# A four-part model on one core: feed-forward norms summed on ACT, a quantiser that takes the maximum twice, a column ahead of the gates, and a new plan

## The chip, the cores and the metric

The kernel runs on one core of a Trainium2 chip. The metric is the time on the device in microseconds (us), median of a few runs. The core's engines work side by side, each through its own list of instructions in order: PE (matrix products; PEld is its loading of weights), DVE (vector), ACT (functions of single elements), POOL (general), and SP, which here only issues the transfers (DMA). PE writes its results to PSUM, a small memory of eight banks of 128x512 floats; all else lives in SBUF. An engine waits for another at semaphores.

## The reference

The input x is 16 sequences of 512 tokens with 128 channels, in float32. Four residual blocks follow each other, each on the layer norm of x (mean and variance over the 128 channels).

```python
x = x + _L0_attn_a_ref(_layernorm(x), ...)   # four layers of RWKV
x = x + _L0_ffn_ref(_layernorm(x), w_gate, w_up, w_down)
x = x + _L0_attn_b_ref(_layernorm(x), w_qkv, w_out, b_out)   # causal attention, one head of 64
x = x + _L0_ffn_ref(_layernorm(x), w_gate, w_up, w_down)
```

An RWKV layer has a time mix and a channel mix. In the time mix k, v and a gate r are products of mixtures of a token and the one before it; per channel a recurrence over the tokens keeps a running weighted mean of v:

```python
qq = jnp.maximum(pp, ww)
e1, e2 = jnp.exp(pp - qq), jnp.exp(ww - qq)
out = (e1 * aa + e2 * vv) / (e1 * bb + e2)
```

The channel mix squares the relu of a 128 to 512 product, goes back to 128, and gates it. The feed-forward block rounds the inputs of every product to a 4-bit grid, in blocks of 16 along the last axis:

```python
scale = jnp.maximum(jnp.max(jnp.abs(xb), axis=-1, keepdims=True) / 6.0, 1e-12)
idx = jnp.searchsorted(_MID, jnp.abs(xb / scale))
q = _GRID[idx] * jnp.sign(xb / scale) * scale       # grid 0, .5, 1, 1.5, 2, 3, 4, 6
h = jax.nn.silu(fp4_linear(x, w_gate)) * fp4_linear(x, w_up)     # 352 wide
return fp4_linear(h, w_down)
```

## The kernel before

All of x stays in SBUF. A sequence is a tile of 128 tokens by 4 blocks of 128 channels. The stages are `in` (load and the two first norms), `x0` to `x3` (the four RWKV layers, two sequences at a time, eight groups), `ffn1`, `att`, `ffn2` (one sequence at a time) and `out`; `w0` to `w3` and `wf` prepare weights. Each stage of each group is a generator that yields operations with their tiles; where an operation can run on several engines it yields alternatives.

The order on every engine is written by a planner in the kernel, at build time. `Issue.merge` keeps up to 8 generators (`ACTIVE`) in play and picks one operation after the other, by a start time that it works out from cost formulas (in `tt`, `ts`, `act` and others), hop times between engines and free buffers, shifted by ranks of the stages (`RANK`), leads of kinds of operations (`LEAD`), ages and a seeded jitter (`SEEDS`). The result is a fixed program order for each engine; at run time only semaphores wait. Tiles come from pools: `slots` (s, 128x513), `wides` (w, 128x1028), `tinys` (t, statistics and scales) and eight PSUM banks (ps).

Three places matter here.

`ln_stats` takes the sums for a layer norm. DVE takes `bn_stats` of each 128x128 block, small operations combine them, POOL raises the variance to the power -0.5 (`power`), and `normalise` applies scale and bias, on POOL or ACT. A second way lies in the function behind `scratch`: ACT sums x and then the squares of x minus its mean through the accumulator of its activations; DVE scales both.

`quant` rounds to the grid: the maximum of each block of 16, its reciprocal, a product on POOL, then rounding by adding and subtracting a large number (`MAGIC`, or a multiple of the value, `ABOVE`): ACT takes the multiple and a Relu of it less `MAGIC`, DVE adds and subtracts in two passes, and POOL multiplies by the scale. `ffn` calls it on 128x512 for x and on 128x704 in two parts of 352 for h.

`time_mix` computes the recurrence as scans on DVE. In the last of them the weights are s = 0.5 - 0.5 tanh(...) of the token before, and it scans over differences of v plus bias from one token to the next. Tile `t2` holds the tanh and later v, `a2` the differences and the result.

Line numbers of the profile that are helpers: L431 `mm`, L434 `tp` (transposes), L366 `act`, L340 `tt`, L344 `stt`, L355 `ts`, L335 `power`, L409 `scan`, L413 `reduce_max`, L419 `bn_stats`, L425 `memset`, L376 `copy`. Since one line serves many steps, groups are told apart by tile names and shapes.

Of the kernel before, what the change touches and what calls it, by code (L numbers as in the profile page):

```python
# [10 lines left out]
F32 = mybir.dt.float32  # L11
# [3 lines left out]
AF = mybir.ActivationFunctionType  # L15
# [8 lines left out]
D = 64  # L24
# [10 lines left out]
N_SLOT = 22  # L35
N_TINY = 12
# [9 lines left out]
AGE = 15.97  # L46
SWITCH = 89.0

FIRST = 45770.0
AGE_FIRST = 19.9  # L50
AGE_LAST = 9.79
LAST = 7
# [4 lines left out]
    882, 832, 99, 213, 457, 65, 500, 631, 716, 630, 411, 526, 117, 14, 667, 453, 213, 800, 28, 513, 118, 323, 14, 553,  # L57
    825, 916, 944, 652, 176, 713, 814, 499, 482,
# [9 lines left out]
WEIGHT = {"V": 2.491, "A": 0.666, "P": 0.962, "T": 1.0, "D": 1.0, "L": 0.1}  # L68
# [9 lines left out]
    "A ps<-ps 251": -70.2, "A ps<-ps 438": 10.4, "A ps<-ps 571": 66.4, "A ps<-ps,x 571": 1.0, "A ps<-s 199": 98.1, "A ps<-s 386": 59.3,  # L78
    "A ps<-s 519": 35.0, "A ps<-w 386": -10.5, "A ps<-w 518": -28.1, "A s,t<-ps,t 344": 44.6, "A s,t<-ps,t 451": 8.1, "A s,t<-ps,t 557": 80.1,
    "A s,t<-ps,t 664": -29.3, "A s<-ps 158": 6.6, "A s<-ps 265": -24.8, "A s<-ps 371": -35.8, "A s<-ps 478": -13.6, "A s<-ps 663": -94.0,  # L80
    "A s<-s 519": -64.5, "A s<-x,t,t 385": -157.7, "A w<-ps 345": 30.5, "A w<-ps 571": 21.8, "A w<-ps,x 571": 19.8, "A w<-s 519": -103.2,
    "A w<-w 1038": -45.5, "A w<-w 944": -102.7, "A w<-w 945": -29.7, "A x<-ps 131": -19.2, "A x<-ps 158": -51.1, "A x<-s 199": -34.4,
    "A x<-s 519": 2.9, "A x<-s,t,t 385": -60.5, "A x<-x 199": -49.8, "A x<-x 519": -15.8, "D <-x 873": 15.5, "D s<- 430": 88.9, "D s<- 600": -20.0,
    "D s<- 873": -0.5, "D x<- 430": 51.2, "D x<- 873": 50.8, "P s<- 205": -44.8, "P s<-s,s 1226": -38.8, "P s<-s,t 1082": 88.5, "P s<-s,t 353": 32.2,
    "P s<-s,t 778": 27.3, "P s<-x,t,t 426": 28.5, "P t<-t 1634": 7.7, "P t<-t 942": -9.6, "P t<-t,t 158": 12.7, "P t<-t,t 167": 22.1,
    "P w<- 42": 38.0, "P w<-s,w 1226": 50.0, "P w<-w,t 1447": 19.3, "P w<-w,w 1223": 135.0, "P w<-w,w 152": -129.2, "P w<-w,w 2342": 43.2,
    "P w<-x 205": 58.4, "P x<-s,t,t 426": 23.4, "P x<-s,x 1226": 77.6, "P x<-s,x 389": -58.1, "P x<-x 1226": 77.2, "P x<-x 426": 11.9,
    "P x<-x 714": 32.8, "P x<-x,s 1226": 2.1, "P x<-x,x 1082": 39.6, "T ps<- 110": 58.7, "T ps<-s 110": -3.8, "T ps<-s 222": 95.6,
    "T ps<-s,s 110": -22.4, "T ps<-s,s 125": 48.3, "T ps<-s,s 179": -47.5, "T ps<-s,s 222": 21.3, "T ps<-s,s 232": 35.4, "T ps<-s,x 222": -107.1,
    "T ps<-s,x 592": 18.2, "T ps<-w 110": -49.3, "T ps<-w,x 222": 6.6, "T ps<-x,s 859": -13.0, "T ps<-x,w 232": -40.0, "V ps<-ps,w 1130": -121.8,  # L90
    "V ps<-w,ps 602": -29.7, "V s<-ps,s 203": 129.0, "V s<-ps,s 436": 116.3, "V s<-ps,s 603": -30.8, "V s<-ps,s 664": -66.8, "V s<-s 197": 41.2,
    "V s<-s,ps 203": 74.3, "V s<-s,ps 436": 35.3, "V s<-s,ps 603": 21.0, "V t<-ps 203": -3.0, "V t<-ps 336": -3.6, "V t<-ps 470": 54.2,
    "V t<-ps 603": 27.2, "V t<-s 202": -45.8, "V t<-s 203": -8.6, "V t<-s 436": 48.3, "V t<-s 603": -12.1, "V t<-t 120": 18.9, "V t<-t 207": 17.1,
    "V t<-t 270": 29.9, "V t<-t 345": -4.3, "V t<-t 70": 49.5, "V t<-t 74": 46.9, "V t<-t 81": 23.7, "V t<-t 86": 54.8, "V t<-t 92": -18.5,
    "V t<-t 95": -69.9, "V t<-t,t 74": 37.1, "V t<-t,t 78": 19.2, "V t<-w 803": -116.6, "V t<-x 202": -43.8, "V w<-ps 1130": -106.2,
    "V w<-ps,w 1130": 44.4, "V w<-ps,w 436": -41.7, "V w<-ps,w 603": -43.4, "V w<-ps,w 664": -21.7, "V w<-s 336": -11.8, "V w<-w 662": -15.3,
    "V w<-w,ps 436": -34.2, "V w<-w,ps 602": -6.0, "V w<-w,w 71": -10.9, "V x<- 70": 23.1, "V x<-ps 71": -21.7, "V x<-ps,t,x 264": -79.9,
    "V x<-s 136": -43.6, "V x<-s 336": -11.0, "V x<-x 136": -11.5, "V x<-x 336": 12.9, "V x<-x 603": 49.6, "V x<-x 71": 1.7, "V x<-x,ps 603": -76.8,
    "V x<-x,x 603": 76.5,
# [5 lines left out]
    "warm": (-2, 0), "in": (-0.806, 0.421), "w0": (-0.644, 0), "w1": (0.622, 0.147), "w2": (1.351, 0.081), "w3": (1.608, 0), "wf": (2.286, 0),  # L105
    "x0": (-0.078, 0), "x1": (1.222, 0), "x2": (2.04, 0), "x3": (3.568, 0), "ffn1": (3.742, 0.485), "att": (5.354, 0.494), "ffn2": (6.262, 0.674),
    "out": (7.177, 0.552),
# [5 lines left out]
LN_ACT = False  # L113
# [89 lines left out]
class View:  # L203


    def __init__(self, buf, steps=()):
        self.buf, self.steps = buf, steps
        a = self._at(buf.tile)
        self.shape = a.shape
        row = a.ap[0][0]  # L210
        self.lo = a.offset % row if row else 0
        self.spread = any(st == 0 and n > 1 for st, n in a.ap[1:])
        self.hi = self.lo + sum(st * (n - 1) for st, n in a.ap[1:])
        if buf.psum:

            self.lo, self.hi = 0, 1 << 20
# [48 lines left out]
def in_psum(v):  # L265
    return isinstance(v, View) and v.buf.psum
# [41 lines left out]
class Issue:  # L308
# [28 lines left out]
    def tt(self, e, out, a, b, op):  # L337
        n = width(out)
        cost = 70 + 1.042 * n if e == "V" else 110 + (1.9 if any(isinstance(v, View) and v.spread for v in (a, b)) else 2.18) * n + 40 * (n < 64)
        return self.op(e, cost, out, (a, b), lambda: self.eng(e).tensor_tensor(real(out), real(a), real(b), op))  # L340
# [5 lines left out]
    def ts(self, e, out, a, s0, s1, op0, op1=None):  # L346
        n = width(out)
        ptr = is_ap(s0) + is_ap(s1)
        if e == "V":
            cost = 70 + (1.042 if in_psum(a) or in_psum(out) else 0.52) * n + 61 * ptr  # L350
        else:
            cost = (330 + 0.75 * n) if op0 == ALU.mult else 200 + 2.7 * n
        args = (op0,) if op1 is None else (op0, op1)
        two = not in_psum(a) and not in_psum(out)
        return self.op(e, cost, out, (a, s0, s1), lambda: self.eng(e).tensor_scalar(real(out), real(a), real(s0), real(s1), *args), two_port=two)  # L355

    def act(self, out, a, func, bias=None, scale=None, accum=None, note=None, after=()):
        n = width(out)
        cost = (52 if in_psum(a) else 93) + 0.833 * n + 93 * (is_ap(bias) + (is_ap(scale) and not callable(scale)) + is_ap(accum))
        kw = {k: v for k, v in (("bias", bias), ("scale", scale), ("accum_out", accum)) if v is not None}  # L360
        outs = [out] + ([accum] if accum is not None else [])

        def call():
            if note:
                note()
            return self.nc.scalar.activation(real(out), real(a), func, **{k: v() if callable(v) else real(v) for k, v in kw.items()})  # L366

        return self.op("A", cost, outs, (a, bias, scale), call, func.name, after=after)
# [329 lines left out]
class Net:  # L698
# [133 lines left out]
    def time_mix(self, l, xs):  # L832
# [53 lines left out]
        yield S.act(t2.v.flat, c.v.flat, AF.Tanh, scale=0.5, bias=mw)  # L886
# [5 lines left out]
        for j, x in enumerate(xs):  # L892
            if DIFF:

                v, vb = self.ps(), t2[:, j, :]
                p = self.ps()
                sv = p[:, 1:T]
                if not S_LATE:
                    yield S.act(sv, t2[:, j, 0 : T - 1], AF.Copy, scale=-0.5, bias=0.5, after=(c.v,))
                yield from self.project(v.v, W["Wv"], hds[j], after=(c.v,))  # L900
                if S_LATE:
                    vb = self.slot()[:, 0:T] if S_LATE == 2 else vb
                    yield S.act(sv, t2[:, j, 0 : T - 1], AF.Copy, scale=-0.5, bias=0.5, after=(v.v,))
                yield S.act(vb, v.v, AF.Identity, bias=W["bias"][:, 0:1])
                yield Free(v)
                yield S.add("dv", a2[:, j, 1:], t2[:, j, 1:], t2[:, j, 0 : T - 1], ALU.subtract)
                yield S.small(a2[:, j, 0:1], t2[:, j, 0:1], t2[:, j, 0:1], ALU.add)
                yield S.scan(sv, sv, a2[:, j, 1:], 0.0, ALU.mult, ALU.add)
                yield S.stt(sv, to[:, j, 1:], -1.0, sv, ALU.add, ALU.mult)
                yield S.stt(a2[:, j, 1:], t2[:, j, 1:], 2.0, sv, ALU.mult, ALU.add)  # L910
# [195 lines left out]
    def quant(self, v, xn, tiny, parts):  # L1106
# [13 lines left out]

        at = 0
        for n in parts:
# [3 lines left out]
            yield S.act(cc, cc, AF.Relu, bias=self.nmagic[0:p])  # L1126
            yield S.stt(xp, cc, MAGIC, xp, ALU.add, ALU.add)
            yield S.stt(xp, xp, -MAGIC, cc, ALU.add, ALU.subtract)
# [196 lines left out]
def block_kernel(ctx, tc, a, out):  # L1325
# [20 lines left out]
    k.nmagic = k.const.tile([128, 1], F32, name="nmagic")  # L1346
    nc.vector.memset(k.nmagic, -MAGIC)
# [99 lines left out]
```

## Time and profile before

| what | value |
|---|---|
| time, median of 3 runs | 1418.98 us (1418.74 to 1421.64) |
| the profiled execution | 1421.8 us, span 1420.0 us |
| mean granted PE clock | 0.986 |
| PE, DVE, ACT, POOL busy | 1336.0, 1329.2, 1270.6, 1138.0 us |
| instructions | 25100 |
| DMA | 18.48 MB, 13 GB/s in the mean |

The page gives busy time and share by engine, then forty slices of the span, the DMA queues, the chain of work that ended last, and the costliest groups of instructions. In a group, the two numbers after the bar are busy us and the mean ns of one instruction; after the next bar stands the engine's idle time before them and who ended it. The mean duration of an instruction and the time until the next one starts differ, since an engine overlaps neighbours. Transfers take 4% of the DMA engines' time and are spread over the first 35 us, the loading of later weights, x again for the residual after `x3`, and the output.

### The profile page before, as it was taken

The page shows a single profiled execution, that of the slowest core. Times are in us where ns is not written, and L with a number is a line of the kernel's source. Part 1 is how long each engine was busy: PE and PEld are TensorE (multiplying, and loading weights), DVE is VectorE, ACT ScalarE, POOL GpSimd, SP SyncE. Part 2 cuts the span into 40 slices and gives each one's busy share as a digit, 9 for nine tenths or more (in the row PEclk, how much of TensorE's full clock was granted, in tenths as well). Part 3 has the DMA queues.
Part 4 walks back from the last instruction along what each step waited for, and adds up shares of the span by engine and source line. Part 5 has one row for each costly group of instructions (what it writes and reads, how often), then busy time and mean ns, then how long its engine had stood idle before and what let it go on. Part 6 is the DMA issues. An engine that isn't in the chain of part 4 may idle for free.

```text
span 1420.0 us, 25100 instructions
## 1 busy us (share of the span) xinstructions
PE 1336.0 (94%) x8219; PEld 1115.9 (79%) x8219; DVE 1329.2 (94%) x3378; ACT 1270.6 (89%) x2350; POOL 1138.0 (80%) x1653
## 2 busy tenths in 40 slices
PE   1589999999999999999999999999999999999988
PEld 1368888888888888888888888888777776777766
DVE  8999999999999999999989999888999999899997
ACT  5889999999999999998999999988888898788885
POOL 7989897887778889787698877988778777677775
PEclk9799999999999999999999999999999999899998
DMA  5000000000000000000000000001000000000001
GB/s 160 1 15 2 0 2 1 1 3 10 14 13 6 3 1 24 1 1 1 1 1 1 16 16 23 24 16 31 1 1 1 1 16 1 15 1 24 8 16 45
DMA packets 31330, 18.48 MB, mean 13 GB/s; under 512 B 1568, under 2 KB 30176, under 8 KB 31200
## 3 DMA queue, kind: packets, MB, share of 16 engines
q1 hardware_dynamic: 31200, 16.89, 4.1%
q8 instruction: 65, 1.06, 0.3%
q14 instruction: 65, 0.53, 0.1%
HBM read 12.69 MB, written 4.19 MB: 12 GB/s over the span
## 4 chain that ended last, share of the span: by engine, by line
PE 57%; DVE 21%; ACT 16%; issue 2%; POOL 2%; SPq 1%; DMA 0%; DVEq 0%; ACTq 0%; POOLq 0%
PE ps L431 51%; ACT s L366 7%; PE ps L434 6%; DVE w L344 4%; ACT ps L366 4%; ACT w L366 3%; DVE w L409 3%; DVE w L340 2%; DVE s L344 2%; DVE t L419 2%; ACT L366 2%; DVE ps L409 1%; DVE t L344 1%; DVE t L413 1%; DVE x L340 1%
## 5 line engine op out<-in xcount | busy, mean ns | idle before, releaser
L366 ACT ACTIVATE s<-ps 128x512 f32<-128x512 f32 (+4 forms) x592 | 330.4, 581 | 46.9 <-PE ps L434 27.5
L431 PE MATMUL ps<-Wcv,s 128*128 128x128 f32 x2048 | 279.7, 275 | 1.2 <-ACT s L366 1.1
L355 POOL TENSOR_SCALAR s<-x,t 128x128 f32<-128x128 f32 x556 | 251.6, 464 | 34.5 <-DVE t L344 15.8
L431 PEld LDWEIGHTS ps<-Wcv,s 128*128 128x128 f32 x2048 | 266.0, 192 | 15.3 <-ACT s L366 2.4
L340 POOL TENSOR_TENSOR w<-w,t 128x704 f32<-128x704 f32 x128 | 176.8, 1388 | 45.2 <-DVE w L344 13.2
L431 PE MATMUL ps<-w,Wck 128*128 128x512 f32 x768 | 207.3, 407 | 4.1 <-DVE w L344 1.5
L335 POOL TENSOR_TENSOR t<-t,nhalf 128x8 f32<-128x8 f32 (+1 forms) x120 | 171.9, 1435 | 41.3 <-DVE t L344 40.0
L434 PE MATMUL ps<-ident,s 128*128 128x128 f32 x873 | 158.9, 280 | 35.3 <-ACT s L366 21.5
L431 PEld LDWEIGHTS ps<-w,Wck 128*128 128x128 f32 x768 | 137.3, 189 | 43.0 <-POOL w L340 5.4
L419 DVE BATCH_NORM_STATS2 t<-x 128x6 f32<-128x128 f32 x704 | 160.4, 277 | 0.4
L366 ACT ACTIVATE s<-s 128x512 f32<-128x512 f32 x248 | 156.3, 637 | 1.5
L434 PEld LDWEIGHTS ps<-ident,s 128*128 128x128 f32 x873 | 107.9, 143 | 58.5 <-ACT s L366 27.5
L366 ACT ACTIVATE ps<-w 128x511 f32<-128x511 f32 (+1 forms) x256 | 134.9, 535 | 7.6 <-POOL w L340 3.3
L431 PE MATMUL ps<-w,Wk 128*128 128x512 f32 x384 | 130.5, 434 | 4.3 <-DVE w L344 4.3
L344 DVE SCALAR_TENSOR_TENSOR w<-ps,w 128x352 f32<-128x352 f32 (+1 forms) x192 | 108.8, 569 | 13.4 <-ACT ps L366 12.0
L431 PE MATMUL ps<-w,Wv 128*128 128x512 f32 x384 | 117.6, 418 | 3.5 <-DVE w L340 3.5
L340 POOL TENSOR_TENSOR x<-x,s 128x512 f32<-128x512 f32 x80 | 103.4, 1295 | 18.0 <-DVE s L344 10.5
L431 PE MATMUL ps<-w,Wr 128*128 128x512 f32 x384 | 114.1, 419 | 1.9 <-DVE w L344 1.8
L344 DVE SCALAR_TENSOR_TENSOR w<-w,ps 128x352 f32<-128x352 f32 (+1 forms) x192 | 107.8, 565 | 1.1
L431 PE MATMUL ps<-wd,s 128*128 128x128 f32 (+1 forms) x768 | 106.6, 278 | 2.4 <-ACT s L366 2.2
L431 PEld LDWEIGHTS ps<-wd,s 128*128 128x128 f32 (+1 forms) x768 | 96.1, 191 | 12.4 <-ACT s L366 5.6
L431 PE MATMUL ps<-wg,s 128*128 128x352 f32 x256 | 100.5, 475 | 3.9 <-ACT s L366 3.7
(143 smaller groups left out, 3439.7 us busy)
## 6 DMA issues: line engine op xcount, KB each, us to landing
s<-in_x SPq DMA_DIRECT2D x32, 256.0 KB, 3.1
out<-x SPq DMA_DIRECT2D x16, 256.0 KB, 2.3
s<-in_Wck SPq DMA_DIRECT2D x4, 256.0 KB, 3.4
Wcv<-in_Wcv SPq DMA_DIRECT2D x4, 256.0 KB, 3.2
s<-in_Wk SPq DMA_DIRECT2D x4, 64.0 KB, 2.2
s<-in_Wv SPq DMA_DIRECT2D x4, 64.0 KB, 2.4
s<-in_Wr SPq DMA_DIRECT2D x4, 64.0 KB, 2.0
Wo<-in_Wo SPq DMA_DIRECT2D x4, 64.0 KB, 3.4
```

The costliest lines, as they stand in the source:

```text
L335: return self.op("P", 250 + 173 * width(out), out, (a,), lambda: self.nc.gpsimd.tensor_tensor(real(out), real(a), half, ALU.pow), brief=True)
L340: return self.op(e, cost, out, (a, b), lambda: self.eng(e).tensor_tensor(real(out), real(a), real(b), op))
L344: return self.op("V", cost, out, (a, s, b), lambda: self.nc.vector.scalar_tensor_tensor(real(out), real(a), real(s), real(b), op0, op1))
L355: return self.op(e, cost, out, (a, s0, s1), lambda: self.eng(e).tensor_scalar(real(out), real(a), real(s0), real(s1), *args), two_port=two)
L366: return self.nc.scalar.activation(real(out), real(a), func, **{k: v() if callable(v) else real(v) for k, v in kw.items()})
L409: return self.op("V", cost, out, (a, b), lambda: self.nc.vector.tensor_tensor_scan(real(out), real(a), real(b), init, op0=op0, op1=op1))
L413: return self.op("V", cost, out, (a,), lambda: self.nc.vector.tensor_reduce(real(out), real(a), AX.X, ALU.max, **kw))
L419: return self.op("V", 202, out, (a,), lambda: self.nc.vector.bn_stats(real(out), real(a)))
L431: return self.op("T", cost, out, (lhsT, rhs), lambda: self.nc.tensor.matmul(real(out), lhsT=real(lhsT), rhs=real(rhs), start=start, stop=s ...
L434: return self.op("T", 110, out, (a,), lambda: self.nc.tensor.transpose(real(out), real(a), ident), after=after)
```

## The change

Four things, in one edit.

1. `LN_ACT` becomes true: the norms of both feed-forward stages take the way behind `scratch`. For a sequence ACT does four Identity passes with an accumulator, DVE scales the sums, ACT does four Square passes with bias and accumulator, DVE scales those, POOL takes the power, DVE multiplies. The four `bn_stats` and the small operations after them go. The normalised tile serves as scratch.
2. In `quant` the Relu on ACT goes (and the constant `nmagic`). Both DVE passes compute max(multiple, `MAGIC`) minus the value.
3. In `time_mix` the tanh is written into `t2` with one column ahead of each sequence, which POOL sets to 1.0. The PSUM tile of s, the differences, the scan and the two products then run over all 512 columns, and the separate addition that made column 0 of the result goes.
4. The pools have one slot and three tinys more, some cost formulas and all parameters of the plan have other values, so the whole program order is another, and so is the choice of engine where there are alternatives.

```diff
-N_SLOT = 22
-N_TINY = 12
+N_SLOT = 23
+N_TINY = 15
...
-AGE = 15.97
-SWITCH = 89.0
+AGE = 17.82
+SWITCH = 108.0
...
-WEIGHT = {"V": 2.491, "A": 0.666, "P": 0.962, "T": 1.0, "D": 1.0, "L": 0.1}
+WEIGHT = {"V": 1.726, "A": 1.05, "P": 0.639, "T": 1.0, "D": 1.0, "L": 0.1}
...
-LN_ACT = False
+LN_ACT = True
...
-        cost = (52 if in_psum(a) else 93) + 0.833 * n + 93 * (is_ap(bias) + (is_ap(scale) and not callable(scale)) + is_ap(accum))
+        base = (43 if in_psum(out) else 68) if in_psum(a) else 76 if in_psum(out) else 106
+        cost = base + 0.833 * n + 93 * (is_ap(bias) + (is_ap(scale) and not callable(scale))) + 18 * is_ap(accum)
...
-        yield S.act(t2.v.flat, c.v.flat, AF.Tanh, scale=0.5, bias=mw)
+        if DIFF:
+
+            ahead = View(t2)[:, 0 : G * (T + 1)].rearrange("p (g t) -> p g t", g=G)
+            yield S.memset("P", ahead[:, :, 0:1], 1.0)
+            yield S.act(ahead[:, :, 1 : T + 1], c.v, AF.Tanh, scale=0.5, bias=mw)
...
-                yield S.act(vb, v.v, AF.Identity, bias=W["bias"][:, 0:1])
-                yield Free(v)
-                yield S.add("dv", a2[:, j, 1:], t2[:, j, 1:], t2[:, j, 0 : T - 1], ALU.subtract)
-                yield S.small(a2[:, j, 0:1], t2[:, j, 0:1], t2[:, j, 0:1], ALU.add)
-                yield S.scan(sv, sv, a2[:, j, 1:], 0.0, ALU.mult, ALU.add)
-                yield S.stt(sv, to[:, j, 1:], -1.0, sv, ALU.add, ALU.mult)
-                yield S.stt(a2[:, j, 1:], t2[:, j, 1:], 2.0, sv, ALU.mult, ALU.add)
+                yield S.act(vb, v.v, AF.Identity, bias=W["bias"][:, 0:1])
+                yield Free(v)
+                yield S.add("dv", a2[:, j, :], vb, ahead[:, j, 0:T], ALU.subtract)
+                yield S.scan(p.v, p.v, a2[:, j, :], 0.0, ALU.mult, ALU.add)
+                yield S.stt(p.v, to[:, j, :], -1.0, p.v, ALU.add, ALU.mult)
+                yield S.stt(a2[:, j, :], vb, 2.0, p.v, ALU.mult, ALU.add)
...
             yield S.act(cc, xp, AF.Abs, scale=ABOVE)
-            yield S.act(cc, cc, AF.Relu, bias=self.nmagic[0:p])
-            yield S.stt(xp, cc, MAGIC, xp, ALU.add, ALU.add)
-            yield S.stt(xp, xp, -MAGIC, cc, ALU.add, ALU.subtract)
+            for _ in range(2):
+                yield S.stt(xp, cc, MAGIC, xp, ALU.max, ALU.subtract)
```

## The prediction

> **What bounds the kernel now.** I read the busy times first, then the chain of work that ended last, then busy time in three stretches, then the groups by shape, and last the order of time on one engine.
>
> ```profile
> PE 1336.0 (94%) x8219; PEld 1115.9 (79%) x8219; DVE 1329.2 (94%) x3378; ACT 1270.6 (89%) x2350; POOL 1138.0 (80%) x1653
> ```
>
> Four engines are between 80% and 94% busy, so no single one explains the time. The chain's shares by engine:
>
> ```profile
> PE 57%; DVE 21%; ACT 16%; issue 2%; POOL 2%; SPq 1%; DMA 0%; DVEq 0%; ACTq 0%; POOLq 0%
> ```
>
> TensorE leads, but DVE and ACT hold over a third. I cut the span at two marks: 306.0 us, where DVE starts the 25th of 64 scans `w<-wdec,ps` (one for each layer and sequence), and 971.5 us, its last `s<-ps,nowr,s` (last channel mix). The columns are length, then PE, PEld, DVE, ACT, POOL busy.
>
> ```profile
> 0.00:306.00 306.00, 251.81 (x1452) 209.73 (x1453) 296.55 (x774) 268.47 (x453) 263.27 (x415) 0.97 0.08 21
> 306.00:971.50 665.50, 655.89 (x4195) 570.96 (x4194) 617.13 (x1359) 630.56 (x1064) 540.65 (x833) 1.00 0.03 10
> 971.50:1420.00 448.50, 428.34 (x2575) 335.19 (x2573) 415.54 (x1248) 371.56 (x835) 334.11 (x407) 0.98 0.04 12
> ```
>
> In A (0 to 306) DVE is busy 97% and PE 82%: DVE sets the pace. In B (to 971.5) PE is busy 98.6%: PE. In C (to the end) PE shows 95.5%, DVE 92.7%; but PE's rows overlap, and priced by step (below) its work in C is only 381 us of 448.5. There DVE's 417 is the largest load, and neither ACT nor POOL is near.
>
> The groups that the change touches (count, then busy us, mean ns):
>
> ```profile
> L419 DVE BATCH_NORM_STATS2 t<-x 128x6 f32<-128x128 f32 x704 | 160.4, 277 | 0.4
> L366 ACT ACTIVATE s<-s 128x512 f32<-128x512 f32 x248 | 156.3, 637 | 1.5
> L366 ACT ACTIVATE ps<-ps,nmagic 128x352 f32<-128x352 f32 x129 | 67.9, 529 | 1.7
> L340 DVE TENSOR_TENSOR w<-w 128x1 f32<-128x1 f32 x48 | 25.1, 523 | 2.8 <-ACT w L366 2.6
> L366 ACT ACTIVATION_READ_ACCUMULATOR s<-ps,t 128x1 f32 x64 | 13.1, 204 | 0.0
> L366 ACT ACTIVATE ps<-ps,nmagic 128x512 f32<-128x512 f32 x32 | 21.4, 668 | 0.3
> L340 POOL TENSOR_TENSOR s<-s 128x512 f32<-128x512 f32 x8 | 8.3, 1042 | 2.4 <-ACT s L366 2.3
> ```
>
> A mean duration overstates what an instruction occupies, since neighbours overlap. So I price by the step from a start to the next start where the engine does not idle:
>
> ```profile
> 1036.77 1.11 DVE L344 SCALAR_TENSOR_TENSOR x<-ps,t,x 128x128 f32<-128x128 f32 x4
> 1037.81 0.27 DVE L344 SCALAR_TENSOR_TENSOR t<-t 128x4 f32<-128x4 f32 x2
> 1038.01 0.86 DVE L419 BATCH_NORM_STATS2 t<-x 128x6 f32<-128x128 f32 x4
> 1038.82 0.95 DVE L340 TENSOR_TENSOR w<-w,ps 128x352 f32<-128x352 f32 x2
> ```
>
> ```profile
> 1046.22 0.54 ACT L366 ACTIVATE ps<-ps,nmagic 128x352 f32<-128x352 f32 x1
> 1046.66 0.51 ACT L366 ACTIVATE s<-x,t 128x128 f32<-128x128 f32 x1
> ...
> 1059.35 0.37 ACT L366 ACTIVATE s<-ps,t 128x128 f32<-128x128 f32 x1
> 1059.61 0.19 ACT L366 ACTIVATION_READ_ACCUMULATOR s<-ps,t 128x1 f32 x1
> 1059.71 0.46 ACT L366 ACTIVATE s<-ps,t 128x256 f32<-128x256 f32 x1
> ```
>
> Four statistics take 0.81 us: 0.20 each. The Relu takes 0.44 (0.45 over all), and reading an accumulator adds 0.10 to its activation, not the 0.204 of its row.
>
> **The change part by part.** Counts are differences of the two programs' instructions by engine; steps are means over the timeline of before.
>
> *Feed-forward norms.* DVE loses 128 statistics: 128 x 0.20 = 25.6 us. Of its `t<-t 128x4` arithmetic it keeps 64 fewer, x 0.12 = 7.5, and gains 16 small adds, 1.9. ACT gains 128 Identity and 128 Square passes over 128x128, each with an accumulator read. No row shows this from SBUF. The nearest: an SBUF copy of 128x128 (`Wr<-s`) steps 0.21, a pointer bias adds 0.09 (`ps<-ps,nmagic` 0.45 against 0.36 for `w<-ps`, both 128x352), the read 0.10. So 0.31 and 0.40, together 91 us. Bounds: reads wholly hidden 65, whole durations instead of steps (0.30 and 0.39, plus 0.204) 141. I take 91, since the timeline shows the 0.10. The upper end would put ACT in C (below) at 408 instead of 367 us, 4 over DVE: +4 us on the time; the lower end changes nothing.
>
> *Quantiser.* ACT loses the Relu: 129 x 0.45 + 32 x 0.57 = 76 us. DVE's two passes stay two, of the same shapes; the second now reads PSUM first, 0.44 against 0.43: nothing. A maximum might price otherwise than an addition; no row shows a difference between ALU operations (`s<-s,ps` with add and multiply and `s<-ps,s` with two additions, both 128x512, both step 0.60), so 0.
>
> *Column ahead.* The 64 column-0 adds go, 48 of them on DVE, where they step 0.485 in the mean: 23.3 us (one lasts 4.32 us, the shortest 0.14). The lower bound is 48 x 0.07 = 3.4, if the wait in them only moves to the next instruction. I take 23, because what follows them, scans and PSUM arithmetic, has no such tail in the trace (`w<-wdec,ps` 1185 to 1219 ns, `w<-ps,w` 665 to 692). They lie in A (17) and B (31), so the lower bound would cost A some 7 us. The 32 new memsets on POOL step 0.08: 2.5. Scans and products grow by one column of 511: nothing.
>
> *New plan.* 46 squares go from ACT (0.52, 24 us) to POOL (1.02, 47 us), and 29 normalisations from ACT (0.39, 11 us) to POOL (0.43, 12 us). POOL's small adds fall by 69 (14 us). SP issues the same 92 rows, but thirteen x loads instead of two now precede layer 1's weights, which are used only when layer 0 has finished for a group; layer 0's work hides it, and without that cover one such load of 2.0 to 3.4 us would be exposed.
>
> Totals: DVE 25.6 + 7.5 - 1.9 + 23.3 = 54 less; ACT 76 + 24 + 11 - 91 = 20 less; POOL some 48 more; PE the same 5,860 program instructions.
>
> POOL's addition is where a rule speaks against the change. DVE's small `t<-t` operations step 0.14 for 128x8 and 0.12 for 128x4 against a shortest 0.08; 565 of them step about 31 us more in all than at their shortest. The Trainium skill (SBUF — State Buffer, Who interferes with whom) says that a DVE instruction with two SBUF inputs contends with a GpSimd instruction that reads SBUF. By it, POOL's 4% more work lengthens those waits by 4%, an estimate of 1.3 us on DVE; by the rows alone nothing is added.
>
> *By stretch.* I weighted the instructions of both programs up to the same marks with these steps (PE: 0.237 for a 128x512 pass, 0.222 for 128x128 in its two rows, 0.593 for 128x352, 0.110 for a transpose).
>
> - A: DVE 292 to 297, because work from behind the mark (three more `w<-ps,w`, two `w<-w,wdec`, two norm products and the like) fills the 8 us of column adds that vanish; PE 226 to 239, so PE arrives 13 us of work further. DVE sets A: 306 + 5 = 311 us. POOL's 8 us more has 43 us of idle time to go into.
> - B: PE 668 to 645, DVE 597 to 552, ACT 588 to 557, POOL 488 to 518. PE sets B: 665.5 x 645/668 = 643 us. DVE's and ACT's relief is worth nothing here.
> - C: DVE 417 to 404 (20 less for statistics, 5 for small arithmetic, some more quantiser work that B had), PE 381 to 391, ACT 358 to 367, POOL 341 to 348. If DVE's losses stay, 448.5 - 13 = 435.5. PE comes close behind, so of its 10 us more between nothing and all come back; I take half: 440 us.
>
> Sum 311 + 643 + 440 = 1394, 26 less than the span of 1420.0. The profiled execution took 1421.8 us, 2.8 over the median of 1418.98; so 1418.98 - 26 gives 1393 us.
>
> **The rivals.**
>
> *Slower: ACT and DVE wait for each other in the new norms.* Each of 32 norms has DVE scale ACT's sums, ACT square with that, DVE scale again: 64 times DVE's queue can stop for ACT, and the quantiser's passes and PSUM products queue behind it; PE waits for those. Rows of such waits (`DVE w L344 <- ACT ps L366: 12.0, 21, 1.7`) give 0.57 us each: 64 x 0.57 = 36 in C, so 1429. It decides from 26/64 = 0.41 us each. Against it: eight threads are interleaved, and DVE now idles 34 of C's 448 us for everything together.
>
> *C does not shorten.* If C's losses come from dependencies of single sequences and not from DVE's load, C stays at 448.5 plus 5: 311 + 643 + 453.5 gives 1408, or 1407 by the median. For it: PE's own idle rows in C name ACT more than DVE.
>
> *The plan's gain in B is not there.* PE's 13 us of lead at 306 is spent again on waits, B stays 665.5: 311 + 665.5 + 440 = 1416.5, within 0.2% at 1415.5 or a little more.
>
> *Better than forecast.* PE's lead shows in A as well (DVE loses its idle 9 us) and C, too, is filled to 97% by DVE's load, 416 us: 302 + 643 + 416 = 1361, 1360 by the median. Against it: PE's 391 us there would also have to run at 94%, where it now has 85%.
>
> **How the numbers follow.** 0.2% (2.8 us) is what a measurement can tell from no change. Forecast 0.50 (1380 to 1404); C not shorter 0.17; better 0.11; B without gain 0.07, of which 0.05 within 0.2%; slower 0.15. Faster: 0.50 + 0.17 + 0.11 + 0.02 = 0.80; same 0.05; slower 0.15. The range takes in the better case down to 1370 and C not shorter, and reaches to 1424 into the slower one; that leaves out 0.12 above and 0.05 below.
>
> **What would show it.** DVE busy near 1275, no `w<-w 128x1` row, 576 statistics `t<-x`; 128 + 128 accumulating activations with a READ_ACCUMULATOR step near 0.10; POOL near 1185; PE's work unchanged; the last `s<-ps,nowr,s` near 954 us. The forecast is wrong if DVE's waits for ACT at the new norms total over 26 us, if the accumulating pairs step nearer 0.55 than 0.35 (ACT then at 408 in C, the new bound), or if the first 300 us lose PE's lead.

## The result and the profile after

The changed kernel takes 1412.14 us (median of 20 runs, 1408.02 to 1421.44), the kernel before beside it 1419.11 us (20 runs). The ratio is 0.995, 95% interval 0.9939 to 0.996: faster by half a per cent, where 1.8% were forecast. The direction is right, the size is not: 7 us came of 26.

The profiled execution of the changed kernel was its longest, 1421.44 us. So I read durations from it, and stretches from a run with the same order whose profiled span is 1412.1 us and whose median (1412.09 us) equals the changed kernel's. In that run, called the typical run here, DVE does 23 us less work in C (below, the product of gate and up over half the columns); wherever that matters, the changed kernel's own profile stands beside it.

Busy time, and the shares of the chain that ended last, of the changed kernel:

```profile
PE 1336.9 (94%) x8219; PEld 1124.5 (79%) x8219; DVE 1311.1 (92%) x3151; ACT 1252.1 (88%) x2633; POOL 1183.5 (83%) x1686
PE 61%; DVE 18%; ACT 10%; POOL 7%; issue 2%; DMA 1%; SPq 0%; DVEq 0%; ACTq 0%; POOLq 0%
```

POOL's 1183.5 is as forecast (1185), PE's unchanged. DVE lost 18 us where 54 were forecast. The groups that answer to those shown of before (count, busy us, mean ns, idle before):

```profile
L421 DVE BATCH_NORM_STATS2 t<-x 128x6 f32<-128x128 f32 x576 | 128.8, 277 | 0.3
L368 ACT ACTIVATE s<-s 128x512 f32<-128x512 f32 x202 | 127.2, 633 | 2.8
L368 ACT ACTIVATE s<-x 128x128 f32<-128x128 f32 x128 | 38.2, 305 | 0.0
L368 ACT ACTIVATION_READ_ACCUMULATOR s<-x 128x1 f32 x128 | 25.2, 197 | 0.0
L368 ACT ACTIVATION_READ_ACCUMULATOR s<-x,t 128x1 f32 x128 | 24.7, 193 | 0.0
L341 POOL TENSOR_TENSOR s<-s 128x512 f32<-128x512 f32 x54 | 56.2, 1045 | 11.1 <-ACT s L368 11.1
L356 DVE TENSOR_SCALAR t<-t 128x4 f32<-128x4 f32 x64 | 12.3, 200 | 1.4 <-ACT s L368 1.1
L356 DVE TENSOR_SCALAR t<-t 128x44 f32<-128x44 f32 x64 | 19.2, 300 | 0.4
```

128 statistics are gone, the Relus and the one-column additions too. Of the last two rows, the first is new: the scaling of ACT's sums. DVE idles 1.4 us before it in all, 1.1 of them for ACT, so the rival in which DVE and ACT stop each other at the norms did not come. The second was there before, with 199 ns: it grew by half, though nothing about it was changed.

The stretches of the typical run, cut at the same two marks (length, then PE, PEld, DVE, ACT, POOL busy). In the changed kernel's own, longest profile they are 326.5, 640.9 and 452.3 us, so its extra 7 us lie in A.

```profile
0.00:319.40 319.40, 266.43 (x1564) 225.83 (x1565) 307.51 (x790) 279.50 (x471) 281.23 (x449) 0.98 0.08 22
319.40:960.40 641.00, 631.82 (x4018) 552.66 (x4017) 587.69 (x1232) 597.19 (x1051) 557.52 (x843) 1.00 0.04 11
960.40:1412.10 451.70, 435.47 (x2641) 343.50 (x2639) 396.35 (x1131) 374.40 (x1113) 344.37 (x395) 0.99 0.04 10
```

| stretch | before | forecast | typical after | miss |
|---|---|---|---|---|
| A | 306.0 | 311 | 319.4 | +8 |
| B | 665.5 | 643 | 641.0 | -2 |
| C | 448.5 | 440 | 451.7 | +12 |

The sum of the misses is the 18 us between the forecast span of 1394 and 1412. So A and C are to be explained, C above all: DVE has less work there (409.5 us busy in the changed kernel's own profile, 415.5 before) and C is no shorter. A stretch's length moves by some 3 us from run to run: C takes 445.4 us in a run of the order before in which nothing in C was edited (the column with one input, below), against the 448.5 of the table. B's shortening is for the most part a move of work across the marks: PE is busy 24 us less in B than before, 15 us more in A and 7 more in C.

### The profile page after: what moved, and what is told of

It is laid out like the page before. It is cut to its first block, busy times and chain, and to the rows that moved or that the text cites. A ratio compares the mean times of both kernels' runs of the same rounds, so it can differ in the third digit from the quotient of the medians.

```text
span 1419.7 us, 25086 instructions
## 1 busy us (share of the span) xinstructions
PE 1336.9 (94%) x8219; PEld 1124.5 (79%) x8219; DVE 1311.1 (92%) x3151; ACT 1252.1 (88%) x2633; POOL 1183.5 (83%) x1686
## 4 chain that ended last, share of the span: by engine, by line
PE 61%; DVE 18%; ACT 10%; POOL 7%; issue 2%; DMA 1%; SPq 0%; DVEq 0%; ACTq 0%; POOLq 0%
PE ps L433 56%; ACT s L368 7%; PE ps L436 6%; DVE w L345 3%; DVE w L411 2%; DVE s L345 2%; DVE t L421 2%; POOL s L356 2%; POOL x L341 2%; POOL t L334 1%; ACT w L368 1%; DVE t L345 1%; ACT ps L368 1%; DVE ps L411 1%; POOL w L341 1%
## 5 line engine op out<-in xcount | busy, mean ns | idle before, releaser
L368 ACT ACTIVATE s<-ps 128x512 f32<-128x512 f32 (+3 forms) x592 | 327.2, 576 | 54.9 <-PE ps L436 33.7
L356 POOL TENSOR_SCALAR s<-x,t 128x128 f32<-128x128 f32 x585 | 263.6, 463 | 39.2 <-DVE t L345 12.1
L345 DVE SCALAR_TENSOR_TENSOR w<-ps,w 128x352 f32<-128x352 f32 (+1 forms) x320 | 170.3, 546 | 12.9 <-ACT ps L368 11.5
L436 PE MATMUL ps<-ident,s 128*128 128x128 f32 (+1 forms) x873 | 160.8, 279 | 16.9 <-ACT s L368 12.4
L368 ACT ACTIVATE ps<-w 128x352 f32<-128x352 f32 (+2 forms) x256 | 131.7, 533 | 16.2 <-POOL w L341 9.2
L436 PEld LDWEIGHTS ps<-ident,s 128*128 128x128 f32 (+1 forms) x873 | 107.9, 142 | 36.2 <-ACT s L368 14.8
L368 ACT ACTIVATE s<-s 128x512 f32<-128x512 f32 x202 | 127.2, 633 | 2.8
L421 DVE BATCH_NORM_STATS2 t<-x 128x6 f32<-128x128 f32 x576 | 128.8, 277 | 0.3
L433 PE MATMUL ps<-w,Wk 128*128 128x512 f32 x384 | 118.2, 423 | 1.9 <-DVE w L345 1.4
L368 ACT ACTIVATE s<-x,t 128x128 f32<-128x128 f32 x247 | 103.0, 439 | 4.1 <-DVE t L356 2.6
```

The source lines that it names most:

```text
L345: return self.op("V", cost, out, (a, s, b), lambda: self.nc.vector.scalar_tensor_tensor(real(out), real(a), real(s), real(b), op0, op1))
L421: return self.op("V", 202, out, (a,), lambda: self.nc.vector.bn_stats(real(out), real(a)))
L433: return self.op("T", cost, out, (lhsT, rhs), lambda: self.nc.tensor.matmul(real(out), lhsT=real(lhsT), rhs=real(rhs), start=start, stop=s ...
L436: return self.op("T", 110, out, (a,), lambda: self.nc.tensor.transpose(real(out), real(a), ident), after=after)
```

## The experiments

In the first three groups every engine's list of instructions keeps its order, that of the changed kernel or that of before; only what an instruction does, or how often it is issued, differs. Where I give a difference it is of medians, against 1412.14 for the changed kernel and against 1419 (1418.97 to 1419.81 beside the runs) for the one before.

### Work added to the changed kernel, one engine at a time

DVE takes 128 further statistics that nobody reads; ACT takes the quantiser's multiple twice; PE makes 384 transposes twice; POOL makes 159 normalisations twice. One edit stands for all:

```diff
-            yield S.act(cc, xp, AF.Abs, scale=ABOVE)
+            yield S.twice(S.act(cc, xp, AF.Abs, scale=ABOVE))
```

> The changed kernel with its program order kept on every engine, and in each of the 32 feed-forward norms four statistics on DVE whose result nobody reads: 128 x 0.20 = 26 us more on DVE, 21 of them after the last channel mix (stretch C). Theory 1, that of the prediction, that DVE's load sets C: 18 to 26 us slower than the changed kernel (about 1430 to 1438 us). Theory 2, that C is set by PE's flow and by what single sequences wait for, so that DVE has slack there: 0 to 6 us slower (1412 to 1418).

> The changed kernel with its order kept, and the quantiser's activation issued twice in a row: 167 more on ACT, 128 x 0.39 + 32 x 0.53 = 67 us, some 58 of them in C, where ACT's load by steps goes from 367 to 425 us, over DVE's 404. Theory 1: ACT becomes the bound of C, some 20 us slower (1432). Theory 2: ACT's 78 us of idle time in C take most of it, but PE waits for ACT in C more than for any other engine, so 10 to 35 us slower, more than for the same us on DVE.

> The changed kernel with its order kept, and each transpose of the feed-forward's inner tile issued twice: 384 x 0.11 = 42 us more on PE, 36 of them in C. Theory 1: PE's load in C goes from 391 to 427, past DVE's 404, so 20 to 25 us slower (1432 to 1437). Theory 2, C follows PE: 34 to 42 us slower (1446 to 1454).

> The changed kernel with its order kept, and on POOL the first of each four normalisations issued twice: 159 x 0.42 = 67 us more on POOL, spread over all stretches, about as much as the change itself gave POOL (48 us). Theory 1: POOL is idle 236 us of 1420 and takes it for 0 to 8 us (1412 to 1420). Theory 4: slope near that of the others, 0.6 to 1, so 40 to 67 us more; also the two-input small operations of DVE then wait longer, by 5 us and more in sum.

| added, by the steps | time, us | ratio to before (95%) | us of time for each us added |
|---|---|---|---|
| DVE +26 | 1440.32 | 1.0151 (1.013 to 1.0172) | 1.1 |
| ACT +67 | 1471.18 | 1.0354 (1.0326 to 1.0382) | 0.88 |
| PE +42 | 1444.42 | 1.0164 (1.0137 to 1.0191) | 0.76 |
| POOL +67 | 1460.60 | 1.0291 (1.0277 to 1.0305) | 0.72 |

Added work costs most of its length at each of these places, also on POOL, which is idle for 236 us of the span, and on ACT with 168. By its expectation the first run alone would have spoken for DVE's load (28 us for 26), but the other three engines, with smaller loads, cost nearly as much, so these runs do not tell the theories apart. In all four the addition stands in a sequence's own path: the statistics, for one, come just before the scaling that ACT's squares wait for. So each lengthens that path as well as the engine's load; work added beside every path was not tried.

### Work taken away from the changed kernel

First the squares on POOL (54 of 128x512), of which only 64 columns are done; then DVE's product of gate and up in the feed-forward, 176 of 352 columns:

```diff
-                    yield S.tt("V", hq, hq, up[:, 0:I], ALU.mult)
+                    hh, uh = hq[:, 0:176], up[:, 0:176]
+                    yield S.less(S.tt("V", hq, hq, up[:, 0:I], ALU.mult), lambda hh=hh, uh=uh: self.nc.vector.tensor_tensor(real(hh), real(hh), real(uh), ALU.mult))
```

> The changed kernel in its own order, but the squares on POOL (54 of 128x512) do only 64 of the 512 columns, which leaves the rest unsquared; some 46 us less on POOL, about what the new plan had given it. Theory 1 (POOL's 48 us, which the prediction had put at nothing, are what kept the forecast from coming): by the 0.72 us for each us that adding POOL work cost, 33 us less, near 1379. Theory 2 (POOL's load is hidden, as predicted; the missing part lies in the order itself and in DVE's waits): 1408 to 1413. Theory 3 (in a fixed order work taken away returns less than added work costs): 1390 to 1406.

> The changed kernel in its own order, but the product of gate and up in the feed-forward is done for 176 of its 352 columns, which leaves the other half ungated; 128 passes lose about 0.2 us each, 26 us less on DVE, nearly all in the last third. Theory 1 (the last third is set by DVE's load, as the prediction took it): 20 to 26 us less, 1386 to 1392. Theory 2 (it is set by waits between engines in the fixed order): 0 to 8 us less, 1404 to 1412. With theory 1 the 20 us that DVE's busy time did not fall would explain the miss.

The squares' row in the first and the product's in the second (61.9 us at full width in the changed kernel):

```profile
L993 POOL TENSOR_TENSOR s<-s 128x64 f32<-128x64 f32 x54 | 16.0, 296 | 21.9 <-ACT s L368 21.0 <-POOL s L993 0.7
```

```profile
L1212 DVE TENSOR_TENSOR w<-w,ps 128x176 f32<-128x176 f32 x128 | 39.1, 322 | 7.4 <-PE ps L437 4.3 <-ACT w L368 1.0 <-ACT ps L368 0.8
```

POOL less by 40 us: 1405.19 us (0.99, 0.9878 to 0.9922), 7 less. That is far from the 33 of the first theory, and at the weak end of what the third had (1390 to 1406). So of POOL's 48 us these squares explain some 7 of the missing 19, no more. By the profiles A is 2.0 us shorter, where the cut takes 8.5 us of POOL's busy time, and B 6. DVE less by 23 us: 1412.09 us (0.9943, 0.9925 to 0.996), nothing. DVE's load does not set C.

Then in addition PE's up product over the same 176 columns; both cuts also in the kernel before; and, in the changed kernel alone, DVE's gate of the channel mix (64 passes, 256 of 512 columns), which lies in A and B:

```diff
-                            yield S.mm(o[:, 0:I], xb, w[:, 0, :])
+                            if o is up:
+                                yield S.less(S.mm(o[:, 0:I], xb, w[:, 0, :]), lambda o=o[:, 0:176], xb=xb, w=w[:, 0, 0:176]: self.nc.tensor.matmul(real(o), lhsT=real(xb), rhs=real(w), start=True, stop=True))
+                            else:
+                                yield S.mm(o[:, 0:I], xb, w[:, 0, :])
```

> The changed kernel in its own order, as in the run with less DVE work, and in addition the up product on PE computes only the 176 columns that are still used: 128 products lose half of their 0.59 us, some 30 to 36 us less on PE, nearly all in the last third. Theory 1 (PE sets the last third, and the prediction's price of its work there was what misled): 20 to 33 us less, 1379 to 1392. Theory 2 (no engine's load does, only waits in the fixed order): 0 to 8 us less, 1404 to 1412.

> The kernel before in its own order, with the product of gate and up done for 176 of its 352 columns (the other half stays ungated): some 23 us less on DVE in the last third. Theory 1 (DVE set the last third before, as the prediction took it, and the change made PE the bound): 15 to 23 us less, 1396 to 1404. Theory 2 (it did not set it before either): 0 to 5 us less, 1414 to 1419.

> The kernel before in its own order, as the run with less DVE work in it, and in addition the up product on PE computes only the 176 columns that are still used: 30 to 36 us less on PE in the last third. If PE sets that third before as well: 20 to 33 us below the run without it. If DVE sets it: 0 to 8 us below.

> The changed kernel in its own order; in the channel mix the gate is applied to 256 of 512 columns (the rest is left ungated): 64 passes lose about 0.3 us each, 19 us less on DVE, about 7 of them in the first third and 12 in the second. If DVE sets the first third and PE the second, as predicted: 5 to 8 us less, 1404 to 1407, all of it before the 25th scan. If DVE's load counts in both: 12 to 19 us less, 1393 to 1400. If in neither: 1410 to 1414.

> The changed kernel in its own order with all four cuts at once: squares on POOL for 64 of 512 columns, the gate of the channel mix for 256 of 512, gate times up for 176 of 352 and the up product on PE for those 176, which leaves the rest undone; some 40 us less on POOL, 40 on DVE, 33 on PE. If the loads hold the time together: clearly more than the sum of the separate effects (7, 3 and 7 us), 1365 to 1385. If the waits of the written order hold it: about that sum, 1393 to 1399.

| taken away | time, us | ratio to before (95%) | against the same without this cut |
|---|---|---|---|
| changed: DVE -23 in C | 1412.09 | 0.9943 (0.9925 to 0.996) | 0 |
| changed: and PE -37 in C | 1405.01 | 0.9894 (0.9875 to 0.9914) | -7 |
| before: DVE -23 in C | 1416.54 | 0.9984 (0.9969 to 0.9999) | -2 |
| before: and PE -37 in C | 1413.62 | 0.9957 (0.9939 to 0.9974) | -3 |
| changed: DVE -17 in A and B | 1408.98 | 0.9926 (0.9907 to 0.9945) | -3 |
| changed: POOL -40 in A and B | 1405.19 | 0.99 (0.9878 to 0.9922) | -7 |
| changed: all of these | 1396.48 | 0.9844 (0.9822 to 0.9865) | -16 |

The sizes are the differences of the rows' busy times. The cut in the channel mix fits none of its three expectations well: 1.3 us come in A and 4.4 in B by the profiles, so DVE's load is no clear bound in A either. In both kernels, C is set neither by DVE's load nor by PE's: 60 us of work less on the two give 7 in the changed kernel and 5 before. (ACT's and POOL's load in the changed kernel's C was not cut.) Nor do the loads hold the time together, each hiding behind the others: all cuts at once give 16, where the separate ones add up to 17. What work taken away returns (nothing to 0.2 us for each us) is much less than what work added costs.

### The parts alone, in the order of before

The 48 column additions that DVE had are issued as a product with 2, which has one input; then the maximum is taken twice and the Relu not issued at all; then both:

```diff
-                yield S.small(a2[:, j, 0:1], t2[:, j, 0:1], t2[:, j, 0:1], ALU.add)
+                yield S.double(a2[:, j, 0:1], t2[:, j, 0:1])
...
-            yield S.act(cc, cc, AF.Relu, bias=self.nmagic[0:p])
-            yield S.stt(xp, cc, MAGIC, xp, ALU.add, ALU.add)
-            yield S.stt(xp, xp, -MAGIC, cc, ALU.add, ALU.subtract)
+            yield S.silent(S.act(cc, cc, AF.Relu, bias=self.nmagic[0:p]))
+            yield S.stt(xp, cc, MAGIC, xp, ALU.max, ALU.subtract)
+            yield S.issued_as(S.stt(xp, xp, -MAGIC, cc, ALU.add, ALU.subtract), S.stt(xp, cc, MAGIC, xp, ALU.max, ALU.subtract))
```

> The kernel before with its order kept; the 48 column additions that run on DVE are issued as a multiplication by 2, with one input instead of two, same result. Theory 1, that of the prediction: the waits inside them (23 us less the bare 48 x 0.07) vanish, DVE is busy some 18 to 20 us less, and the first 306 us become about 6 us shorter; time 5 to 8 us less than before. Theory 3: the additions only stood where DVE would have waited for POOL anyway; other two-input operations of DVE wait instead, DVE's busy time falls by 0 to 8 us and the time stays within 2 us.

> The kernel before with its order kept; the quantiser takes the maximum twice and the 167 Relus on ACT are not issued, all else as it was: 76 us less on ACT by steps, some 66 of them in the last stretch. Theory 1, the prediction: the last stretch is set by DVE's load and ACT's relief is worth nothing: 0 to 5 us less than before. Theory 4, formed from the runs that added work (26 us on DVE cost 28, 67 us on ACT cost 59, 42 us on PE cost 32): in a fixed order an operation's time counts on every engine, because the orders interlock; the Relu is on the way from product to rounding as well. Then 30 to 60 us less.

> The kernel before in its own order, with its 48 column additions on DVE issued as a product with 2 (one input) and the quantiser's maximum taken twice without the Relu. If the two gains add up: 13.5 and 3.5 us less, 1402. If ACT's relief becomes worth something once DVE is relieved: 1390 to 1398. If the second adds nothing: 1405 to 1406. In each case less than the changed kernel's 1412.

The column with one input, its row and its first two stretches:

```profile
L374 DVE TENSOR_SCALAR w<-w 128x1 f32<-128x1 f32 x48 | 7.0, 145 | 3.0 <-ACT w L366 2.9
```

```profile
0.00:300.30 300.30, 249.85 (x1452) 209.74 (x1453) 289.25 (x774) 268.02 (x453) 263.93 (x415) 0.97 0.08 22
300.30:958.60 658.30, 654.09 (x4195) 570.79 (x4194) 606.42 (x1359) 630.26 (x1064) 542.49 (x833) 1.00 0.03 10
```

The 48 rows fall from 25.1 to 7.0 us, and the time from 1419.04 to 1405.55 us (0.99, 0.9883 to 0.9918): 13.5 us, more than the whole change gives. The wait vanishes and does not move to a neighbour: DVE's busy time falls by 17.6 us (1329.2 to 1311.6). A is 6 us shorter and B 7 (4 to 7 against the runs of this order in which A and B are nearly unedited, where B takes 662 to 666), although PE is busy over 98% of B: the prediction's "worth nothing here" was wrong for this wait. It stood in the middle of a sequence's own chain, between the differences and the last scan.

The profile of before shows what such a wait was worth. Matched with the instructions by their times, the pieces of the chain of work that ended last hold 13.1 us of the 25.1 of these additions, 17 of the 48, 5.3 us in A and 7.8 in B. The longest, first as the chain has it, then on DVE's timeline, then what POOL did meanwhile:

```profile
646.20 4.32 DVE w L340
```

```profile
646.20 4.32 DVE L340 TENSOR_TENSOR w<-w 128x1 f32<-128x1 f32 x1
```

```profile
645.90 2.37 POOL L340 TENSOR_TENSOR w<-w,w 128x1024 f32<-128x1024 f32 x1
648.23 1.03 POOL L340 TENSOR_TENSOR w<-w 128x511 f32<-128x511 f32 x1
649.23 1.27 POOL L340 TENSOR_TENSOR w<-s,w 128x512 fp32r<-128x512 f32 x1
```

Without the 167 Relus and their 76 us of ACT: 1415.65 us (0.999, 0.9975 to 1.0006), at most 4 us; ACT's relief is worth next to nothing, as predicted. Both parts: 1404.10 us (0.989, 0.9867 to 0.9914), between the column alone (1405.5) and the sum of the two (1402); the interval holds both. This version leaves nothing out of the computation, and its median is 8 us below the changed kernel's, with none of the new norms and none of the new plan.

### The same work in another order

Four kernels are planned anew: the three edits with the formulas and parameters of before (and the larger pools); the parameters of after with the three edits undone; and each of the two kernels with other seeds for the jitter and nothing else, as in

```diff
-    387, 333, 29, 789, 10, 184, 541, 594, 396, 428, 701, 992, 530, 325, 125, 213, 547, 520, 89, 289, 990, 948, 911, 232,
-    569, 134, 787, 257, 934, 392, 658, 379, 669,
+SEEDS = [101, 118, 135, 152, 169, 186, 203, 220, 237, 254, 271, 288, 305, 322, 339, 356, 373, 390, 407, 424, 441, 458, 475, 492, 509, 526, 543, 560, 577, 594, 611, 628, 645]
```

> The three edits (norm sums on ACT, maximum twice, column ahead) and the larger pools in the kernel before, with its cost formulas and parameters, so the planner orders the new program by the old numbers. If the new plan is worth its place: 10 to 40 us slower than the changed kernel. If the edits carry all and the plan is luck: within 10 us of the changed kernel's 1412, either side.

> The changed kernel's parameters, cost formulas and pools with the three edits undone: the old program in a new order. Theory 4 and a plan fitted to its program: 10 to 40 us slower than before (1429 to 1460). If the plan is the better half of the change: at or below 1419.

> The changed kernel with other seeds for the planner's jitter and nothing else changed, so the same work in another order. Theory 1 (the time is that of the work by stretch and the order matters little): 1407 to 1418. Theory 2 (the parameters were fitted to one program, and every other order is worse): 1430 to 1480, as with the two re-planned kernels.

> The kernel before with other seeds for the planner's jitter and nothing else changed. If its parameters are fitted to one program as those of the changed kernel are: 1440 to 1490. If only the changed kernel is so sensitive: 1412 to 1430.

| kernel | time, us | ratio to before (95%) |
|---|---|---|
| edits, parameters of before | 1468.82 | 1.0347 (1.0332 to 1.0361) |
| parameters of after, edits undone | 1482.64 | 1.0439 (1.0413 to 1.0465) |
| changed kernel, other seeds | 1457.14 | 1.026 (1.0239 to 1.0282) |
| kernel before, other seeds | 1466.13 | 1.0322 (1.0298 to 1.0345) |

The changed kernel with other seeds (the three stretches):

```profile
0.00:333.40 333.40, 274.08 (x1602) 232.34 (x1603) 309.61 (x794) 289.68 (x485) 290.74 (x451) 0.97 0.07 20
333.40:974.70 641.30, 625.46 (x3968) 547.11 (x3967) 578.98 (x1225) 594.45 (x1056) 546.27 (x818) 0.99 0.04 11
974.70:1451.90 477.20, 450.47 (x2653) 350.23 (x2651) 415.64 (x1141) 384.44 (x1123) 343.85 (x388) 0.97 0.03 10
```

The work is nearly the same (a few operations move to another engine), and the order costs 45 us; in the profile 14 lie in A and 25 in C, where the engines are busy within some 20 us of what they were. The kernel before loses as much (46). In these four runs, parameters and seeds did well only for the program that they came with. With the same other seeds the change is worth 9 us (1466 to 1457), about what it is worth with its own (7); beside a spread of 45 us between orders, one other draw does not show that this is more than chance.

## What C is made of

If no load sets C, its chain may show what does. The chain of work by line within C: before, then in the typical run of the changed order. The shares are of C.

```profile
by line: PE ps L431 49.8%; PE ps L434 10.8%; ACT ps L366 8.2%; ACT s L366 7.2%; DVE w L344 5.2%; DVE t L413 3.6%; issue 2.5%; DVE w L340 2.1%; ACT w L366 1.4%; DVE t L416 1.4%; DVE x L340 1.4%; DVE t L344 1.2%; DVE t L419 1.0%; DVE s L340 0
658 pieces in order of time: start us, us, what
```

```profile
by line: PE ps L437 49.8%; ACT s L368 15.1%; PE ps L440 9.1%; ACT ps L368 3.1%; ACT w L368 3.1%; issue 2.4%; DVE t L419 2.1%; DVE t L356 2.1%; DVE s L345 1.6%; DVE w L345 1.6%; ACT L368 1.4%; POOL w L341 1.4%; DVE x L345 1.0%; POOL s L341 0
```

Before, the chain changes hands 658 times in 448.5 us, every 0.7 us; DVE holds 83 us of it when all pieces are added up (18%), PE 61%. An engine can be busy 93% of a stretch and yet be on its chain for less than a fifth. I had not read this view by stretch, and it speaks against "DVE sets C" before any run. It does not make PE the bound either: PE's up product holds 38 us of that chain, and the cut above, which took 38% of it away, gave 3 us. After, DVE falls to 56 us (49 in the changed kernel's own profile), and ACT's work on `s` rises from 7.2% (32 us) to 15.1% (68 us; 14.0% in the changed kernel's own profile). At the same time ACT's work on `ps`, which had the Relus, falls from 8.2% to 3.1%, and over the whole span ACT's share falls from 16% to 10%; ACT's rise is C's alone. Matched with the instructions, the chain holds 32 us of the new norms' passes and their reads of the accumulator (30 in the changed kernel's own profile); before, it held 4.7 us of DVE's statistics and 19 us of Relus. Of the four longest pieces of ACT on `s` in that chain (3.39, 2.69, 2.56 and 2.42 us) the last three lie on the new norms' passes, wholly or for the most part. One of them, as the chain has it (start, length, instructions), and ACT's timeline at that place:

```profile
981.87 2.69 ACT s L368 x14
```

```profile
981.77 0.39 ACT L368 ACTIVATE s<-x,t 128x128 f32<-128x128 f32 x1
982.06 0.19 ACT L368 ACTIVATION_READ_ACCUMULATOR s<-x,t 128x1 f32 x1
982.15 0.39 ACT L368 ACTIVATE s<-x,t 128x128 f32<-128x128 f32 x1
982.45 0.19 ACT L368 ACTIVATION_READ_ACCUMULATOR s<-x,t 128x1 f32 x1
```

It goes on so for seven squares. They step 0.39, where 0.40 was forecast. Both the Identity and the Square passes of a norm must be through before its power can start. So by the chain, the relief of DVE's queue was paid for with a longer latency of each feed-forward norm. That these passes are what keeps C at 452 is an inference from the chain; a kernel with the old norms and everything else of the change was not run, so how much the new norms alone cost stays open.

A second entry of that chain is a small DVE operation, one of the rows that grew. DVE, then POOL, at that place:

```profile
966.65 2.85 DVE L356 TENSOR_SCALAR t<-t 128x32 f32<-128x32 f32 x1
```

```profile
965.84 1.39 POOL L341 TENSOR_TENSOR w<-w,t 128x704 f32<-128x704 f32 x1
967.18 1.27 POOL L341 TENSOR_TENSOR x<-x,s 128x512 f32<-128x512 f32 x1
968.42 1.04 POOL L341 TENSOR_TENSOR s<-s 128x512 f32<-128x512 f32 x1
```

It ends at 969.50, POOL's run of three at 969.46. The next one of its kind, on 128x44, takes 0.12 us.

## Why the prediction was right and wrong

- **Statistics, accumulator reads, Relu, POOL's new work**: right as durations. 576 statistics at 0.20; pairs of 0.30 (0.20 and 0.10) and 0.39 against 0.31 and 0.40; POOL 1183.5 against 1185.
- **Column ahead, 23 us on DVE**: right that the waits vanish; the one-input run gives 18 of the 23, since 7 us of instruction remain there. In A, where DVE's rows lose 7.3 us, the time loses 6, as DVE's pace there had it. Wrong in B, where it had been put at nothing and gave 4 to 7.
- **Maximum twice, ACT's 76 us**: put at nothing for the time, measured 0 to 4.
- **B, 643**: 641. PE is busy here nearly without a break before and after (all but 9.6 and 9.2 us), and its busy time in B fell by 24 us where 23 of work had been forecast. That the column's relief would count for nothing was wrong, so some of the agreement is luck.
- **A, 311**: 319. DVE is busy 307.5 us in A, 11 more than before, where 5 more had been forecast, and idle 11.9 us instead of 9.5. The step "POOL's 8 us more has 43 us idle to go into" does not hold up: POOL holds 21 us of A's chain before and 65 in the changed kernel's profile (89 in the typical run), half of it in the powers and the normalisations. The squares hold only 1 us of A's chain, which may be why 8.5 us less of them gave no more than 2.0 there. No run cut the other rows of POOL in A, so how much of A's 8 is POOL and how much the new order stays open.
- **C, 440**: 452. This is the step that failed: "DVE's 417 is the largest load", so "DVE's losses stay, 448.5 - 13". Largest load and bound are not the same. 23 us less of DVE in C gave 2 us before and nothing after, 37 us less of PE gave 3 and 7. Nor did DVE lose the 13: in the changed kernel's own profile it is busy 6 us less in C than before. The rival "C does not shorten", with the cause that came nearest (dependencies, not DVE's load), said 453.5 and a time of 1407; it had got 0.17.
- **DVE 54 us less**: 18 came. Small operations on `t` took more time: `t<-t 128x44` 199 to 300 ns, `t<-t 128x8` 215 to 242 ns. By the Trainium skill (SBUF — State Buffer, Who interferes with whom) I had estimated 1.3 us for POOL's added work. The runs do not show that rule's effect of POOL's amount of work: with POOL's squares cut the 288 rows of `t<-t 128x8` take 55.0 us, but in runs of the same order with POOL's work whole they take 55.2 to 65.0. What they show is an effect of the order: `t<-t 128x44` takes 199 to 229 ns in the six runs of the order before and 253 to 342 in the ten of the changed order, also where the squares' cut brings POOL back to 1144 us (288 ns). The same section of the Trainium skill says that a `tensor_scalar` in a two-port mode blocks behind GpSimd (POOL) as well, which I had not used. The 2.85 us above fit it, though no run shows the mode, and the wait went through three instructions.
- **Slower, by waits of DVE for ACT in the new norms**: DVE's idle time before the scaling of ACT's sums totals 1.4 us and not 36. But the same norms came onto the chain in another way, by their length.
- **The new plan**: the forecast weighed what each engine does and let the order follow. Another order is worth 45 us in either kernel, several times the change.

Put together: in the order of before the column with one input and the maximum give 15 us. The changed kernel, which has the maximum and no such column at all, its new norms and 48 us more for POOL, gives 7. The squares' part of the difference of 8 is up to 7 by the cut; the rest lies in the norms, POOL's other rows and the order, which these runs do not separate.

## What to carry to other kernels

In a program whose order is written out and tied by semaphores, do not price a relief by busy time: here a stretch with DVE 93% busy returned 0 to 2 of 23 us. Ask first how much of the very rows that will go lies on the chain of work that ended last. The column additions held 13.1 us of it, and relieving them gave 13.5; DVE's product of gate and up held 9.6, of which the cut took 37%, and gave 2. In every cut here this came nearer than the busy time, but it is a guide and not a price. The Relus held 19 us and gave 4 at most, and PE's up product 50 us (42 after the change), of which the cut took 38% and gave 3 (7): something else must have held the time nearly as long. The squares on POOL held 3 us and gave 7.

Work added in a sequence's path costs most of its length on any engine, idle or not (0.72 to 1.1 us for each us here), so a shift of work from a full engine to an idle one is not free. A wait inside a dependency chain can be worth more than a larger saving of load: 18 us of column waits gave 13.5 us, 76 us of ACT gave 4 at most. And where another order of nearly the same work moves the time by 45 us, a gain of 7 says little about the edits themselves.

## What was not expected of the hardware

- An addition of one column with two inputs lasted 523 ns in the mean (48 rows), a product with a constant at the same place 145 ns.
- A small DVE operation beside POOL can wait for more than the one POOL instruction under way: 2.85 us behind three instructions, ending 0.04 us after the last. In the kernel before the column addition of 4.32 us ends 0.02 us after a third POOL instruction, and one `t<-t 128x8` of 1.79 us likewise. In the changed kernel's profile all 28 such operations (`t<-t`, no reductions or reciprocals) that last over 0.6 us end 0.02 to 0.05 us after a POOL instruction does. Eight of them last through the whole of at least one POOL instruction that started after them, the longest 5.54 us. In 10 of the 28 POOL's next instruction follows without a gap, so DVE does not always need a gap in POOL's run to get in; what decides stays open.
- Halving a DVE pass from 352 to 176 columns shortened its row from 503 to 322 ns, and one PE product from 97.3 to 60.4 us for 256 rows: neither in half.
